# The opening of a graph-attention kernel: the first pair's terms by TensorE, the second quarter's values later

## The chip, the cores and the metric

The kernel runs on one core of a Trainium2 chip. The core has a matrix engine (TensorE, PE in the profile, with its weight loads as PEld), a vector engine (VectorE, DVE), an engine for copies and functions (ScalarE, ACT), a general engine (GpSimd, POOL) and a queue engine that issues transfers (SyncE, SP). Each works through its own queue in order and waits on semaphores for the others. The metric is the device time of one execution in microseconds (us).

## What is computed

Two graph-attention layers over 4096 nodes with 8 heads of 32 features, then one transformer layer over the same nodes, with the adjacency as the mask. The change touches only the start of the first graph-attention layer:

```python
def _gat_layer(x, adj_mat, W, a):
    O = W.shape[-1]
    Wh = jnp.einsum('nd,hdo->hno', x, W)
    src = jnp.einsum('hno,ho->hn', Wh, a[:, :O])
    dst = jnp.einsum('hno,ho->hn', Wh, a[:, O:])
    e = jax.nn.leaky_relu(src[:, :, None] + dst[:, None, :], 0.2)
    e = jnp.where(adj_mat[None, :, :] > 0, e, NEG_INF)
    alpha = jax.nn.softmax(e, axis=-1)
    out = jnp.einsum('hnm,hmo->hno', alpha, Wh)
    return jnp.transpose(out, (1, 0, 2)).reshape(N, -1)
h = jax.nn.elu(_gat_layer(x, adj_mat, W1, a1)) + x
out = jax.nn.elu(_gat_layer(h, adj_mat, W2, a2)) + h
```

Everything is float32; x is 4096 x 256 and adj 4096 x 4096 (int32).

## The kernel before

**How attention is computed.** The exponent of a leaky sum splits into two products, one for each sign of `src[n] + dst[m]`. So the kernel never makes the 4096 x 4096 scores. It compares `src` of a row n with `-dst` of a column m, gets a tile of signs in 8 bits, masks it with the adjacency, and multiplies the signs and the mask with scaled values of the columns on TensorE. The scaled values are `vst`, in two float16 halves that add up to the float32 number.

**Groups.** The work of a layer is cut into groups `(l, nb, p, g)`: layer, block of 1024 rows, pair of heads, and one eighth of the columns (four tiles of 128 nodes, 512 nodes). These eighths are numbered q in the preparation; the title of the change and this text call the first two quarter 0 and quarter 1. A group needs a tile `t8` of 128 x 2 x 4 x 1024 signs. `compare(i)` makes it for group i: for each of the four column tiles k and both heads j one comparison of 128 x 1024 numbers, on ScalarE (L1114) or on VectorE (L1116), and then one masking operation on VectorE (`mask`, L1129). One operand of a comparison is `s_b`, the row terms `src` of the block's 1024 nodes for the two heads, the same on all 128 partitions. The other is one number per partition, `-dst`, from `terms`. A group's matmuls are L1452; they add into six banks of the accumulator memory (bank0 to bank5) over the eight groups of a pair.

**Preparation of a quarter** (`preparation`, L980) makes the values of 512 nodes:

- features: four transposes of the rows of x for each half of the features (L991), and a copy by ScalarE (L1000, tile `g_ft`)
- values: for each of four tiles of 128 nodes two matmuls of 272 columns (`values_out`, L1005): 256 columns of values and 16 of terms. Then `values_in`: two exponentials, one more and a copy of the terms on ScalarE (L1018 to L1020); the largest value (L1023), the product (L1034) and 32 times the exponentials (L1040) on VectorE. For quarter 1 the product goes to `g_prod`, a pool of two buffers
- split: a cast to float16 (L1046, by ScalarE in the opening) and the rest by GpSimd (L1049). The GpSimd operation releases the `g_prod` buffer
- term rows: one transpose (L1054), a copy by ScalarE into `g_sr` (L1060), a pool with one buffer, and four DMAs to the DRAM tensor `s_d` (L1063).

**The mask's own path.** Adjacency units of 256 x 512 are loaded (`mask_load`, L858), clipped to 8 bits by VectorE (`mask_clip`, L867), transposed by TensorE (`turn_out`, L892, into one of two banks named turn), copied by ScalarE (`turn_in`, L898) and written to DRAM for later (L901). The three load buffers `g_adj` come free with the clips; each later clip issues one further load (`load_ahead`).

**The opening** (`begin`, L1280) sets by hand the order of PE, ACT, DVE and SP up to the first group. Before the change this order is: the loads; features of both quarters; the term weights; values of quarter 0 with clips between; quarter 0's term rows; values of quarter 1 with the splits of quarter 0; quarter 1's term rows; `s_fetch` (L1085), two DMAs that read `s_d` back from DRAM with each row repeated over 128 partitions; turns 0 to 3 with clips 4 to 7; `compare(0)`; turns 4 to 7 with the clips of the next column eighth; `compare(1)`. Then the groups follow. The first six groups each also prepare one further quarter: its features, values, term rows, turns and clips are laid between the group's matmuls by position (`side`), in an order that is the same for all engines, and `compare(i + 2)` runs there too.

Before `begin` two small tests run that use the turn banks: L833 and L834 on one, L840 to L846 on the other. They are outside the order written by hand.

Of the kernel before, what the change touches and what calls it, by code (L numbers as in the profile page):

```python
# [8 lines left out]
F32 = mybir.dt.float32  # L9
# [8 lines left out]
ALU = mybir.AluOpType  # L18
# [4 lines left out]
P = 128  # L23
# [661 lines left out]
UP = 32.0  # L685
# [66 lines left out]
def graph_attention(  # L752
# [62 lines left out]
    def turn_bank(shape, dtype):  # L815
        return ps.tile(shape, dtype, name="turn", tag="turn", bufs=2)

    spare = []

    def spare_bank():  # L820

        spare.append(0)
        return ps.tile([P, 512], F32, name=f"bank{(len(spare) - 1) % 6}")

# [153 lines left out]
    def preparation(l, q, bank, first=False):  # L980
# [32 lines left out]
        def values_in(t):  # L1013
            at = G * q + t
            pv = held.pop(("v", t))
            big = some.tile([P, 2, H], F32, name="g_big", bufs=4)
            for i, scale in enumerate((-1.0, -LRELU)):
                nc.scalar.activation(big[:, i, :], pv[:, D + H : D + 2 * H], AF.Exp, scale=scale)  # L1018
            nc.scalar.activation(L.r[:, at, :], pv[:, D : D + H], AF.Exp, scale=LRELU - 1.0)
            nc.scalar.copy(  # L1020
                L.terms[:, :, at, :], pv[:, D : D + 2 * H].rearrange("p (k h) -> p k h", k=2)
            )
            nc.vector.tensor_reduce(  # L1023
                L.tops[:, at : at + 1], pv[:, :D], AX.X, ALU.max, apply_absolute_value=True
            )

            if l == 0 and q != 1:
                if t == 0:
                    held["prods"] = ep.tile([P, G, H, 2, V1], F32, name="ev_broad")
                prod = held[t] = held["prods"][:, t]  # L1030
            else:
                prod = held[t] = some.tile([P, H, 2, V1], F32, name="g_prod")
            by_head = big.rearrange("p i h -> p h i").unsqueeze(3)
            nc.vector.tensor_tensor(  # L1034
                prod[:, :, :, :O],
                pv[:, :D].rearrange("p (h o) -> p h o", o=O).unsqueeze(2).to_broadcast([P, H, 2, O]),
                by_head.to_broadcast([P, H, 2, O]),
                op=ALU.mult,
            )
            nc.vector.tensor_scalar(prod[:, :, :, O:], by_head, UP, None, op0=ALU.mult)  # L1040

        def split(t):
            part = held.pop(t).rearrange("p h i v -> p h (i v)")
# [38 lines left out]
    def take(n):  # L1082
        return [step for _ in range(min(n, len(later))) for step in later.pop(0)]

    def s_fetch(l, nb, p):  # L1085
        s_b = s_p.tile([P, 2, W], F32, name="s_b")
        first, n = STARTS[l][nb] * P, TILES[l][nb] * P
        for j in range(2):
            row = s_d[l][2 * p + j : 2 * p + j + 1, first : first + n]
            nc.sync.dma_start(s_b[:, j, :n], spread(row, [[0, P], [1, n]]))  # L1090
        return s_b
# [5 lines left out]
    def compare(i):  # L1097

        l, nb, p, g = groups[i]
        L, s_b = layers[l], s_of[l, nb, p]  # L1100
        t8 = s8[i] = t_p.tile([P, 2, NW, G, HB], F8, name="t8")
        more = (7, 11, 15, 23, 27, 31) if l == 0 else (3, 7, 11, 15, 19, 23, 27)
        if apart(i):
            u8[i] = [rows_p.tile([P, NW, G, HB], F8, name="g_adj", bufs=3) for j in range(2)]

        def step(k):
            mt = g * G + k
            for j in range(2):
                to = t8[:, j, :, k, :]
                s = s_b[:, j, :].rearrange("p (w n) -> p w n", n=HB)  # L1110
                negd = L.negd[:, mt, 2 * p + j : 2 * p + j + 1]

                if (j == 1 or mt in more) and not (i == 0 and k == 0):
                    nc.scalar.activation(to.bitcast(I8), s, AF.Sign, bias=negd, scale=-1.0)  # L1114
                else:
                    nc.vector.tensor_scalar(  # L1116
                        to, s, negd, -1.0, op0=ALU.is_ge, op1=ALU.mult, saturate=False
                    )

        def mask():  # L1120
            both = t8.rearrange("p j w g n -> p j (w g n)").bitcast(I32)
            m32 = masks[l, nb][g].rearrange("p w g n -> p (w g n)").bitcast(I32)
            for j, u in enumerate(u8.get(i, ())):
                nc.vector.scalar_tensor_tensor(
                    u.rearrange("p w g n -> p (w g n)").bitcast(I32),
                    t8[:, j].rearrange("p w g n -> p (w g n)").bitcast(I32),
                    -1, m32, op0=ALU.bitwise_xor, op1=ALU.bitwise_and,
                )
            nc.vector.scalar_tensor_tensor(  # L1129
                both, m32.unsqueeze(1).to_broadcast(list(both.shape)), SIGNS, both,  # L1130
                op0=ALU.bitwise_or, op1=ALU.bitwise_and,
            )

        return [lambda k=k: step(k) for k in range(G)] + [mask]

    def pair_end(l, nb, p, ev):
# [143 lines left out]
    def begin():  # L1280

        weights_load(0)
        rows_ahead(0, 0)
        rows_ahead(0, 1)

        units = own[: 2 * 2 * NW]
        del coming[: len(units)]
        for k, u in enumerate(units):
            place = None
            if 3 <= k < 7:  # L1290
                place = mask_p.tile([P, 2, G * P], I32, name="mask")
            elif k == 7:
                place = t_p.tile([P, 2, G * P], I32, name="t8")
            mask_load(*u, place)

        def clip(k):
            mask_clip(*units[k], load=False)

        def turn(k):
            mask_turn(*units[k])  # L1300

        def both(use):
            use[0]()
            use[1]()

        (f_0, v_0, part_0, row_0), (f_1, v_1, part_1, row_1) = (
            preparation(0, q, spare_bank, True) for q in range(2)
        )
        for use in f_0 + f_1:
            both(use)  # L1310
        for step in weights_steps(0):
            step()
        for use in v_0[:2]:
            both(use)
        for k in range(2):
            clip(k)
            both(v_0[2 + k])
        both(row_0)
        for k in range(4):
            both(v_1[k])  # L1320
            part_0[k]()
            if k < 2:
                clip(2 + k)
            if k > 1:
                part_1[k - 2]()
        both(row_1)
        s_of[0, 0, 0] = s_fetch(0, 0, 0)
        rows_ahead(0, 2)
        for k in range(4):
            turn(k)  # L1330
            if k < 2:
                part_1[2 + k]()
            clip(4 + k)
        load_ahead(3)
        ahead = turns[0]
        for step in compare(0):
            step()
        for k in range(4, len(units)):
            turn(k)
            mask_clip(*ahead[k - 4])  # L1340
        for step in compare(1):
            step()
# [822 lines left out]
```

## Time and profile before

| | |
|---|---|
| time, median of 3 runs | 3174.34 us (3171.62 to 3174.59) |
| the profiled execution | 3169.78 us, span 3168.0 us |
| TensorE busy | 3073.6 us, 97% of the span |
| VectorE, ScalarE, GpSimd busy | 89%, 84%, 38% |
| granted TensorE clock, mean | 0.996 |
| first matmul of the first group | 40.33 us after the span's start |
| next group's first transposes | 59.94 us |

The page gives shares over the whole span; the opening is the first 1.3% of it. There the timeline is the view to use: one line for each run of like instructions on an engine, with its start, its length, the line of the program, what it writes and reads, how many, and in brackets how long the engine sat idle before it and what ended that. The view of stretches gives busy time by engine in a piece of the span, with the granted clock of TensorE. A float32 matmul stands in the trace as two records.

### The profile page before, as it was taken

How to read it: one execution, taken by the hardware profiler on the slowest of the kernel's cores; microseconds unless marked ns; L12 is line 12 of the kernel's file. 1: busy time of each engine (PE TensorE's matmuls, PEld its weight loads, DVE VectorE, ACT ScalarE, POOL GpSimd, SP SyncE). 2: the span in 40 equal slices, each digit the busy share in tenths (PEclk: the TensorE clock that was granted, in tenths of full speed). 3: DMA queues.
4: the chain of work that ended last, by engine and by line, in shares of the span. 5: the costliest groups of instructions: out<-in, count | busy, mean ns of one | idle time of the engine just before them, and what ended most of it. 6: DMA issues, size and time to landing. Idle time of an engine off the chain costs nothing. (4 is left out here: it accounts for less than half of the span.)

```text
span 3168.0 us, 139144 instructions
## 1 busy us (share of the span) xinstructions
PE 3073.6 (97%) x64076; PEld 2705.3 (85%) x64076; DVE 2809.0 (89%) x3201; ACT 2668.9 (84%) x3177; POOL 1197.6 (38%) x538
## 2 busy tenths in 40 slices
PE   6999999999989999999999999999999999999999
PEld 5899999999889999999985888888888888877766
DVE  7899999989899999999985999999999999998221
ACT  6899999999789999999965888888888888886332
POOL 3300000000330000000002998899988898997110
PEclk8999999999999999999999999999999999999999
DMA  8766555420310312121136010101011010111210
GB/s 256 214 198 206 165 188 152 150 87 22 102 53 23 96 56 86 32 68 56 46 111 173 14 41 18 37 21 34 28 27 33 22 50 8 47 60 56 69 35 22
DMA packets 212034, 250.35 MB, mean 79 GB/s; under 512 B 88240, under 2 KB 132784, under 8 KB 211440
## 3 DMA queue, kind: packets, MB, share of 16 engines
q1 hardware_dynamic: 211440, 241.36, 25.6%
q8 instruction: 503, 8.24, 1.1%
q14 instruction: 91, 0.75, 0.1%
HBM read 198.84 MB, written 42.47 MB: 76 GB/s over the span
## 5 line engine op out<-in xcount | busy, mean ns | idle before, releaser
L1452 PE MATMUL bank<-vst,t 128*128 128x132 f16 x16384 | 1450.7, 219 | 25.3 <-DVE t L1129 25.2
L1936 POOL TENSOR_TENSOR u_both<-u_e 128x1024 f32<-128x1024 f32 x448 | 1049.6, 2384 | 899.5 <-DMA u_k<-half_d 786.4
L1114 ACT ACTIVATE t<-s_b,g_terms 128x1024 int8<-128x1024 f32 x1231 | 1318.9, 1157 | 31.4 <-PE bank L1452 24.4
L1452 PE MATMUL bank<-vst,mask 128*128 128x66 f16 (+1 forms) x10296 | 1344.1, 206 | 0.0
L1452 PEld LDWEIGHTS <-t 128*128 128x128 fp8e4 x16384 | 1183.3, 96 | 39.7 <-DVE t L1129 29.6
L1818 DVE SCALAR_TENSOR_TENSOR u_e<-u_mask,u_ps 128x1024 f32<-128x1024 uint8 x1024 | 1166.1, 1215 | 15.1 <-ACT u_ps L1816 10.2
L1816 ACT ACTIVATE u_ps<-u_ps 128x1024 f32<-128x1024 f32 x1024 | 1030.2, 1009 | 139.7 <-PE u_ps L1809 44.6
L1452 PEld LDWEIGHTS <-mask 128*128 128x128 fp8e4 x10296 | 901.4, 98 | 0.0
L1129 DVE SCALAR_TENSOR_TENSOR t<-mask,t 128x2048 int32<-128x2048 int32 x256 | 589.0, 2301 | 61.3 <-ACT t L1114 51.4
L1809 PE MATMUL u_ps<-u_q,u_k 128*32 128x512 f16 x8192 | 637.4, 381 | 5.9 <-DVE u_e L1818 3.4
L1827 PE MATMUL u_av<-u_e,u_v 128*32 128x128 f32 x16384 | 603.1, 273 | 3.3 <-issue 3.3
L1827 PEld LDWEIGHTS u_av<-u_e,u_v 128*32 128x32 f32 x16384 | 489.4, 110 | 131.6 <-issue 4.8
L1116 DVE TENSOR_SCALAR t<-s_b,g_terms 128x1024 fp8e4<-128x1024 f32 x817 | 587.9, 752 | 2.6 <-DMA s_b<-s_d 2.6
L1049 POOL TENSOR_TENSOR vst<-g_prod,vst 128x528 f16<-128x528 f32 x36 | 59.5, 1669 | 748.2 <-DVE vst L1048 735.6
L1827 PE MATMUL u_dn<-u_both,u_ones 128*32 128x128 f32 x7168 | 282.4, 273 | 0.8 <-POOL u_both L1936 0.8
L1809 PEld LDWEIGHTS <-u_k 128*32 128x32 f16 x8192 | 230.1, 95 | 50.9 <-issue 9.9
L1827 PEld LDWEIGHTS u_dn<-u_both,u_ones 128*32 128x32 f32 x7168 | 214.1, 110 | 42.1 <-POOL u_both L1936 1.7
L2031 ACT ACTIVATE u_hid<-misc,n_b 128x512 f32<-128x512 f32 x64 | 43.9, 687 | 140.2 <-PE misc L2024 140.2
L2044 PE MATMUL misc<-u_k,u_hid 128*128 128x256 f32 x512 | 111.8, 379 | 0.0
L2024 PE MATMUL misc<-ln_cols,u_k 128*128 128x512 f32 x256 | 111.3, 593 | 0.5 <-ACT ln_cols L1548 0.5
L2044 PEld LDWEIGHTS misc<-u_k,u_hid 128*128 128x128 f32 x512 | 96.7, 190 | 13.3 <-issue 0.5
L2024 PEld LDWEIGHTS misc<-ln_cols,u_k 128*128 128x128 f32 x256 | 48.6, 190 | 58.5 <-issue 56.9
(167 smaller groups left out, 1825.0 us busy)
## 6 DMA issues: line engine op xcount, KB each, us to landing
g_adj<-in_adj_dram SPq DMA_DIRECT2D x123, 512.0 KB
s_b<-s_d SPq DMA_DIRECT2D x64, 512.0 KB
mask<-mask SPq DMA_DIRECT2D x128, 256.0 KB
u_mask<-mask SPq DMA_DIRECT2D x32, 512.0 KB
mask<-stage SPq DMA_DIRECT2D x48, 256.0 KB
half_d<-u_halves SPq DMA_DIRECT2D x32, 256.0 KB
u_q<-half_d SPq DMA_DIRECT2D x32, 256.0 KB
rows<-e_x SPq DMA_DIRECT2D x31, 256.0 KB
```

The source lines that it names most:

```text
L1049: nc.gpsimd.tensor_tensor(halves[:, :, 1, :], part, halves[:, :, 0, :], op=ALU.subtract)
L1114: nc.scalar.activation(to.bitcast(I8), s, AF.Sign, bias=negd, scale=-1.0)
L1116: nc.vector.tensor_scalar(to, s, negd, -1.0, op0=ALU.is_ge, op1=ALU.mult, saturate=False)
L1129: nc.vector.scalar_tensor_tensor(both, m32.unsqueeze(1).to_broadcast(list(both.shape)), SIGNS, both, op0=ALU.bitwise_or, op1=ALU.bitwise_and,)
L1452: nc.tensor.matmul(to, left, right, start=k not in opened, stop=last)
L1809: nc.tensor.matmul(ps[r * O : (r + 1) * O, j, :], k_st[c][:, 2 * u + j, at : at + O], q_st[:, h, :], start=True, stop=True,)
L1816: nc.scalar.activation(ps, ps, AF.Exp, scale=SCALE)
L1818: nc.vector.scalar_tensor_tensor(e, mask, 0.0, ps, op0=ALU.not_equal, op1=ALU.mult)
L1827: nc.tensor.matmul(to[j * O : (j + 1) * O, at], lefts[j], es[j // 2][:, j % 2, at], start=first and part == 0, stop=last and part == PARTS ...
L1936: nc.gpsimd.tensor_tensor(both, es_of[i - 1][u], es_of[i][u], op=ALU.add)
L2024: nc.tensor.matmul(ph, w1_sb[:, k, f * P : (f + 1) * P], hn[:, k, :], start=(k == 0), stop=(k == DC - 1),)
L2044: nc.tensor.matmul(po[:, :D], hid[:, f, at : at + P], w2_sb[:, f, :], start=(f == 0), stop=(f == FC - 1),)
```

## The change

- A new helper, `s_spread(q, j, bank)`, makes the row terms of 512 nodes for one head on all partitions: a matmul whose weights are one column of `w_ext` (the term weights of the head) repeated 128 times, with the features of the quarter as the moving operand. ScalarE copies the 128 x 512 result into `s_b`. Four of these replace the first `s_fetch`; the other pairs' terms still go through DRAM.
- Twelve float32 matmuls of the identity by itself (128 columns) into a turn bank stand at the head of TensorE's order. Nothing reads them.
- Quarter 0's values, splits and clips 0 to 3 are followed by turns 0 to 3, the four spreads, clips 4 to 7, three loads. Quarter 1's value matmuls stand behind the spreads on TensorE; their second halves (`values_in`), its splits and the term rows of both quarters stand behind `compare(0)` with its mask, ahead of turns 4 to 7 and `compare(1)`.
- `compare(0)` takes head 0's four tiles first, then head 1's; VectorE does the first two tiles of head 1 rather than one.
- In the opening L1040's multiply is done by ScalarE.
- Banks are given in a list written out, no longer in rotation; the load of quarter 2's rows is issued earlier.

```diff
+    def banks_of(order):
+        left = list(order)
+        def bank():
+            k = left.pop(0)
+            if k is None:
+                return turn_bank([P, 512], F32)
+            return ps.tile([P, 512], F32, name=f"bank{k}")
+        return bank
...
-            nc.vector.tensor_scalar(prod[:, :, :, O:], by_head, UP, None, op0=ALU.mult)
+            if first:
+                nc.scalar.mul(prod[:, :, :, O:], by_head, UP)
+            else:
+                nc.vector.tensor_scalar(prod[:, :, :, O:], by_head, UP, None, op0=ALU.mult)
...
+    def s_spread(q, j, bank):
+        L = layers[0]
+        pt = bank()
+        for c in range(DC):
+            nc.tensor.matmul(
+                pt,
+                L.w_ext[:, c, D + j : D + j + 1].to_broadcast([P, P]),
+                L.ft[q][:, c, :],
+                start=(c == 0),
+                stop=(c == DC - 1),
+            )
+        nc.scalar.copy(s_of[0, 0, 0][:, j, q * HB : (q + 1) * HB], pt)
...
-                if (j == 1 or mt in more) and not (i == 0 and k == 0):
+                if (j == 1 or mt in more) and not (i == 0 and k < 2):
...
+        if i == 0:
+            return [lambda k=k, j=j: step(k, (j,)) for j in range(2) for k in range(G)] + [mask]
...
-            preparation(0, q, spare_bank, True) for q in range(2)
+            preparation(0, q, banks_of(order), True)
+            for q, order in ((0, (0, 1, 4, 5, 0, 1, 2)), (1, (2, 3, None, None, 4, 5, 3)))
         )
+        pt = turn_bank([P, 512], F32)
+        for _ in range(12):
+            nc.tensor.matmul(pt[:, :P], ident_f, ident_f, start=True, stop=True)
         for use in f_0 + f_1:
             both(use)
         for step in weights_steps(0):
             step()
-        for use in v_0[:2]:
-            both(use)
-        for k in range(2):
-            clip(k)
-            both(v_0[2 + k])
-        both(row_0)
+        rows_ahead(0, 2)
+        clip(0)
         for k in range(4):
-            both(v_1[k])
-            part_0[k]()
-            if k < 2:
-                clip(2 + k)
-            if k > 1:
-                part_1[k - 2]()
-        both(row_1)
-        s_of[0, 0, 0] = s_fetch(0, 0, 0)
-        rows_ahead(0, 2)
+            both(v_0[k])
+            if k > 0:
+                part_0[k - 1]()
+            if k in (1, 2):
+                clip(k)
+        clip(3)
+        part_0[3]()
         for k in range(4):
             turn(k)
-            if k < 2:
-                part_1[2 + k]()
-            clip(4 + k)
+        s_of[0, 0, 0] = s_p.tile([P, 2, W], F32, name="s_b")
+        s_bank = banks_of((2, 3, 0, 1))
+        for j in range(2):
+            for q in range(2):
+                s_spread(q, j, s_bank)
+        for k in range(4, len(units)):
+            clip(k)
         load_ahead(3)
         ahead = turns[0]
-        for step in compare(0):
+        comparing = compare(0)
+        for use in v_1:
+            use[0]()
+        for step in comparing[:G]:
+            step()
+        for step in comparing[G:]:
             step()
+        for k in range(4):
+            v_1[k][1]()
+            if k > 0:
+                part_1[k - 1]()
+        both(row_0)
+        both(row_1)
+        part_1[3]()
         for k in range(4, len(units)):
             turn(k)
             mask_clip(*ahead[k - 4])
```

## The prediction

> **What bounds the kernel now.** I read the page first, then the stretches, then ScalarE's, SyncE's and TensorE's timelines of the first 62 us, where the change lies.
>
> From the page, TensorE's share of the chain that ended last, and two of the costliest groups:
>
> ```profile
> PE 45%; POOL 0%; DVE 0%; issue 0%; ACT 0%; ACTq 0%; DVEq 0%
> ...
> L2024 PE MATMUL misc<-ln_cols,u_k 128*128 128x512 f32 x256 | 111.3, 593 | 0.5 <-ACT ln_cols L1548 0.5
> ```
>
> No engine but TensorE has a share that shows, and its page row has it busy for 97% of the span. Nothing behind the opening waits for a clock time: a group starts when the one before it is done. So a microsecond won or lost before the first group should stand at the end, and 6.3 us (0.2% of 3174) is about what this measurement can tell from no change.
>
> Stretches (length, then busy PE, PEld, DVE, ACT, POOL, granted clock, DMA share, GB/s):
>
> ```profile
> 20.80:23.80 3.00, 0.77 (x10) 0.61 (x10) 3.00 (x8) 2.23 (x9) 3.00 (x3) 0.99 0.70 135
> 23.80:40.30 16.50, 3.31 (x24) 2.42 (x23) 11.92 (x17) 8.74 (x15) 5.66 (x5) 0.50 0.75 219
> 40.30:44.20 3.90, 3.87 (x30) 3.75 (x31) 1.89 (x3) 3.90 (x4) 0.00 (x0) 0.50 0.54 169
> 60.00:74.30 14.30, 12.34 (x152) 10.62 (x151) 12.74 (x23) 11.36 (x31) 6.42 (x4) 1.00 0.87 268
> ```
>
> Until 40.3 TensorE is nearly idle. Its clock halves 3.0 us after the last value matmul (20.8) and is back only after 3.9 us of unbroken work. A later group of the opening takes 14.3 us with no engine full: three queues hand work on in a fixed order.
>
> ScalarE's timeline (start, length, line, what, count, idle before):
>
> ```profile
> 23.67 0.25 ACT L1060 COPY g_sr<-bank 32x128 f32<-32x128 f32 x1
> ...
> 34.73 3.23 ACT L1114 ACTIVATE t<-s_b,g_terms 128x1024 int8<-128x1024 f32 x3 [5.04 <-DMA s_b<-s_d]
> ...
> 40.09 5.29 ACT L1114 ACTIVATE t<-s_b,g_terms 128x1024 int8<-128x1024 f32 x5
> 45.28 1.05 ACT L1000 COPY g_ft<-turn 128x512 f32<-128x512 f32 x2
> ```
>
> This is the queue to watch. The terms' row leaves at 23.67, returns over DRAM, and both heads are on the partitions at 34.73. The second comparison starts at 40.09, and behind it waits the copy (45.28) that group 0's features need. I take that 40.09 as the mark.
>
> SyncE and TensorE:
>
> ```profile
> 23.95 1.58 SPq L1063 DMA_DIRECT2D s_d<-g_sr  x4
> ...
> 27.04 0.47 SPq L1496 DMA_DIRECT2D n_be<-in_L_gnn_be_dram  x1
> 27.68 0.82 SPq L1090 DMA_DIRECT2D s_b<-s_d  x2
> ```
>
> ```profile
> 8.09 1.94 PE L991 MATMUL bank<-ident,g_rows 128*128 128x128 f32 x8 [8.09 <-DMA g_rows<-in_x_dram]
> ...
> 59.94 0.60 PE L991 MATMUL turn<-ident,g_rows 128*128 128x128 f32 x4
> ```
>
> Four row DMAs land by 27.68, 2.15 us after the last was issued (25.53). A transpose takes about 0.22 us at 8.09 and 0.11 at 59.94: at 8 us the array ran at half speed, whatever the clock column says for that early time. Value tiles (L1005) go from 1.8 us to 0.91 each at 13.45.
>
> **The change, part by part**, as shifts of the 40.09 mark.
>
> *1. Up to the spread.* Twelve f32 matmuls of 128 columns, two records each, at 0.21 at half speed: 5.1 us from 1.45 (the identity) to 6.6, under the wait for rows that ends at 8.09. They cost nothing; without that cover, 5.1. They may raise the clock: it rose at 13.45, 5.4 us after work began, so 5.1 us may or may not do. If it does, transposes and first values win 2.2 us; bounds 0 and 2.2, I take half. Then VectorE needs, per value tile, 0.34 + 0.60 = 0.94 us (L1023, L1034; L1040 has left it) four times, and two clips of 0.60 between: from 14.11 to 19.1. ScalarE casts (0.54) and copies turns 0 and 1 (0.53 each), which free the two banks for turns 2 and 3 (0.45): the spread, queued behind turn 3, starts at 21.2, less 1.1: 20.1.
>
> *2. The spread.* Head by quarter: four results of two f32 matmuls, two records each, 512 columns: 16 x 0.435 us (111.3/256 above) = 6.96 at full speed; up to 9.5 if a broadcast column keeps records from overlapping (16 x 0.593), which I don't take as 0.435 is what a row of such matmuls showed. From the last value (about 15.3) to 20.1 TensorE has only 16 short transposes, longer than the 3.0 us after which the clock fell: so half speed at first, for the 3.9 us of the row, loss 1.95 (bounds 0, and 2.7 for 5.4 us). The two s_b loads (1 MB) that fall away free nothing that waits: the quarter's own adjacency tiles had landed by 30.7, when their last clip ran without a wait. The copy adds 0.69. Head 1 is there at 20.1 + 6.96 + 1.95 + 0.69 = 29.7, against 34.73: 5.0 won.
>
> *3. First comparisons.* ScalarE has two rather than three: 1.05 + 1.14, then the mask (L1129) 2.29 and hand-overs 0.07: masked at 34.25, against 40.27. 6.0 won; VectorE's six comparisons (0.66) hide, four of them under head 1's spread.
>
> *4. What now stands behind the mask.* In the old order quarter 1's values lay under the DRAM trip. Now ScalarE must do them before turn 4's copy, and every step waits for another engine. From the mask's end: VectorE's tile 0, 0.94; cast 0.54 (at 1.53); GpSimd's subtraction 1.35 (opening's mean for g_prod): 2.9. Only then is one of the two g_prod buffers free, and ScalarE itself waits there, as L1040's multiply now sits in its queue (0.1). Cast 1 (3.55), GpSimd (4.9), multiply, cast 2 (5.55). Row 0's copy 0.16 (finished at 5.8), four issues on SyncE 1.37, landing 2.15: 9.3. Row 1's copy writes the same single g_sr buffer, so it waits for that landing; then 0.16, cast 3 0.54: 10.05. Turns 4 to 7: 2.2 with one wait for TensorE. Second comparison at 34.25 + 12.3 = 46.55. Before, it started 0.18 ahead of the mask's end. So the shift is 46.55 - 40.09 = +6.5. The landing is bounded by 0 and 2.15; SyncE stood still for 0.17 us just before the s_b issue, so I take 2.15. GpSimd's rows span 1.14 to 1.67: -0.4 to +0.6. The eight moved multiplies took VectorE 3.1 us (L1040, 0.17 to 1.08 each); small operations of that size follow each other on ScalarE at 0.06 to 0.1, so beyond the two waits they cost under 0.5, which I leave out.
>
> *5. Queues moved past.* Rows for quarter 2 and the three loads go out earlier, the eight row DMAs later: group 1's last adjacency load, behind them, is issued at about 45.3 and not 41. In the old run its lateness held VectorE 3.19 us. Now VectorE's three comparisons (2.0) end before ScalarE's five (5.3), and the mask comes about 2.9 us earlier after the mark. TensorE then waits no longer for VectorE's product in group 0 (a 0.66 us wait); ScalarE's 1.69 us wait for it may go too. Gain 0 to 2.35; I take TensorE's own, 0.7.
>
> **Sum:** +6.5 - 0.7 = +5.8 us. On the profiled execution (3169.78 run, 3168.0 span) that is 3175.6; the median shown is 4.6 above it: **3180.1**. Bounds: low 5.8 - 1.1 - 1.95 - 2.15 - 0.4 - 1.65 = -1.5; high 5.8 + 1.1 + 0.75 + 2.5 + 0.6 + 0.7 = +11.5. Its own range: 3172.8 to 3185.8.
>
> [...]
>
> **Rivals.**
>
> *Warm-up in the way (slower).* The 12 matmuls need one of two turn banks, and the two start-up tests in the code ahead use the same two. If the bank is theirs until VectorE reads it after the weights (9.0), the matmuls run from 9.1 to 14.2 and features start 6.1 late, at full speed (2.6 won): 3.5 instead of -1.1, so +10.4: 3184.7. For it: L834 ran at 10.10. Against it: the old trace put the tests behind eight transposes, though first in the code, so code order doesn't bind.
>
> *Short tail (faster).* One mechanism: ScalarE's tail behind the mask costs only its work, as buffers free themselves in time. Its own busy time there is about 4 x 0.54 + 2 x 0.3 + 0.3 for quarter 1 and 2.2 for turns: 5.3, and with tile 0's 0.94 it is 6.2 instead of 12.3: +6.5 - 6.1 = +0.4. Group 0, which took 19.6 us (40.33 to 59.94) against 14.3, then starts with its masks early and a fast clock; if it too takes 14.3, -5.3, and with part 1's other half -1.1: -6.0; with the spread at full speed too, -8. I put it at 3167. For it: group 0's excess is in the trace. Against it: the g_prod wait showed even before (0.7 and 0.78 us on VectorE). It decides below a tail of about 7 us.
>
> *It cancels.* The trip saved and the tail pay each other exactly (tail of 6.5): 3174.3.
>
> **Chances and range.** Forecast 60%, of which half beyond 6.3 us, as the sum is near it and the open terms reach further up; warm-up in the way 20%, all slower; short tail 14%, faster; cancels 6%. So slower 0.50, within 0.2% 0.36, faster 0.14. Range 3169 to 3187: it reaches past the slow rival and half-way to the short tail.
>
> **What would show it.** Right: ScalarE idle behind the first mask, waiting for GpSimd, then 3 us before the second g_sr copy; its second comparison near 46.5; s on the partitions near 30; clock 0.5 at the spread's start. Part 1 is wrong if transposes at 8.1 don't take 0.11 or 0.22, or come after 14. The prediction falls if the mark comes before 40, or if the group that starts near 60 has kept nothing of the shift.

## The result, and the profile after

| | before | changed |
|---|---|---|
| time, median of 6 runs each, side by side | 3172.93 us (3169.19 to 3174.59) | 3190.82 us (3189.45 to 3194.68) |
| ratio, with its 95% interval | 1 | 1.0062 [1.0051, 1.0072] |
| profiled execution, span | 3169.78 us, 3168.0 us | 3192.24 us, 3189.4 us |

The change costs 17.9 us. The forecast was 5.8 us, with a range that ended 12.7 us above the median it started from. The direction was right, the size was not.

The same points of the opening in both traces, with the forecast between them (us after the span's start):

| | before | forecast | changed |
|---|---|---|---|
| first transposes of the features (TensorE) | 8.09 | 8.09 | 17.26 |
| spread starts | - | 20.1 | 28.62 |
| head 1's terms on all partitions | 34.73 | 29.7 | 37.4 |
| first mask done | 40.27 | 34.25 | 41.92 |
| second comparison starts on ScalarE (the mark) | 40.09 | 46.55 | 53.01 |
| next group's transposes | 59.94 | +5.8 | 72.88 |

From the page of the changed kernel: busy time by engine, the instruction queue (packets, MB, share), and the shares of the chain that ended last.

```profile
PE 3090.6 (97%) x64116; PEld 2716.9 (85%) x64116; DVE 2809.5 (88%) x3194; ACT 2670.7 (84%) x3188; POOL 1197.4 (38%) x538
...
q8 instruction: 503, 8.24, 1.1%
...
PE 48%; DVE 3%; ACT 2%; issue 1%; DMA 0%; SPq 0%; DVEq 0%; ACTq 0%
```

VectorE and ScalarE now have shares of the chain, 3% and 2%; before, none but TensorE had one that shows. And "issue", time in which an engine waited for nothing that the profile shows, has come up to 1%. These shares don't tell a slower kernel from a faster one: experiment 9, below, the fastest kernel measured here, has PE 47%, DVE 3%, ACT 2% and issue 1%.

The stretches of the changed kernel (same columns as before):

```profile
12.10:17.40 5.30, 5.23 (x26) 5.26 (x27) 0.28 (x3) 0.00 (x0) 0.00 (x0) 1.00 1.05 388
...
28.60:36.80 8.20, 8.20 (x20) 3.80 (x18) 4.88 (x7) 2.63 (x6) 0.38 (x1) 0.87 0.73 225
41.90:52.30 10.40, 2.13 (x18) 1.86 (x19) 6.88 (x12) 4.82 (x19) 4.92 (x4) 0.62 0.02 4
...
73.00:87.30 14.30, 12.35 (x152) 10.63 (x151) 12.73 (x23) 11.36 (x31) 6.42 (x4) 1.00 0.70 234
```

In the first row TensorE is busy for the whole stretch while VectorE, ScalarE and GpSimd do next to nothing: those are the twelve identity matmuls, and everybody waits for them. (24 records in 5.25 us are 0.22 us each; the 16 of the transposes right behind them, in 1.91 us, are 0.12 each. So the matmuls ran at about half speed, though the clock column has 1.00 there.) The third is the tail behind the first mask: 10.4 us in which no engine is full. The last is a later group, the same as before within 0.01 us of TensorE's time.

TensorE's and VectorE's timelines of the changed kernel, around the late start:

```profile
9.20 0.27 PE L845 MATMUL turn<-g_ident_h,g_bits 128*128 128x128 f16 x1 [6.62 <-DVE g_ident_h L811]
12.17 5.25 PE L1336 MATMUL turn<-ident 128*128 128x128 f32 x24 [2.71 <-DVE checks L839]
17.26 1.91 PE L996 MATMUL bank<-ident,g_rows 128*128 128x128 f32 x16
```

```profile
11.27 0.70 DVE L872 TENSOR_SCALAR adj<-g_adj 128x1024 fp8e4<-128x1024 int32 x1 [2.12 <-DMA g_adj<-in_adj_dram]
11.88 0.15 DVE L839 TENSOR_SCALAR checks<-turn 128x1 f32<-128x1 f32 x1
```

The brackets tell the story. The matmuls (L1336) write a turn bank. The start-up check on VectorE (L839) still had to read that bank, and in VectorE's queue it stood behind clip 0 (L872), which waited for its adjacency until 11.27. So 24 records that were to run from 1.45 began at 12.17, and the features began behind them at 17.26 and not at 8.09.

ScalarE's timeline of the changed kernel, behind the mask, and SyncE's:

```profile
42.89 0.63 ACT L1054 CAST vst<-g_prod 128x528 f16<-128x528 f32 x1 [2.52 <-DVE g_prod L1039]
...
44.78 0.23 ACT L1046 ACTIVATE g_prod<-g_big 128x16 f32<-128x16 f32 x1 [0.99 <-POOL vst L1057]
...
47.42 0.25 ACT L1068 COPY g_sr<-bank 32x128 f32<-32x128 f32 x1
50.09 0.25 ACT L1068 COPY g_sr<-bank 32x128 f32<-32x128 f32 x1 [2.42 <-DMA s_d<-g_sr]
...
53.01 5.29 ACT L1136 ACTIVATE t<-s_b,g_terms 128x1024 int8<-128x1024 f32 x5
```

```profile
47.70 3.95 SPq L1071 DMA_DIRECT2D s_d<-g_sr  x8
51.75 0.55 SPq L863 DMA_DIRECT2D g_adj<-in_adj_dram  x1
```

Each wait in a bracket is one that the forecast's step 4 named: the product, GpSimd holding a buffer, the single term-row buffer until its DMAs have landed. Behind the eight row DMAs the late adjacency load goes out at 51.75.

The opening thus accounts for 12.9 us (72.88 - 59.94 = 12.94). That shift stands through both graph layers, 12.65 in the middle (the 129th masking operation, 889.83 against 877.18) and 13.44 at the last (1628.00 against 1614.56). The rest appears where nothing was changed, in the transformer's attention stage. From the first to the last of its sixteen copies into u_den, 1101.69 us before (1801.80 to 2903.49) have become 1108.98 (1815.88 to 2924.86). TensorE's timeline there, the changed kernel and then the one before:

```profile
1887.17 0.52 PE L1865 MATMUL u_dn<-u_both,u_ones 128*32 128x128 f32 x9 [0.86 <-issue]
...
2034.85 0.52 PE L1865 MATMUL u_dn<-u_both,u_ones 128*32 128x128 f32 x10 [0.59 <-issue]
...
2182.90 0.53 PE L1865 MATMUL u_dn<-u_both,u_ones 128*32 128x128 f32 x11 [0.96 <-issue]
...
2852.28 1.04 PE L1847 MATMUL u_ps<-u_q,u_k 128*32 128x512 f16 x7 [4.83 <-issue]
```

```profile
2608.26 0.75 PE L1827 MATMUL u_dn<-u_e,u_ones 128*32 128x128 f32 x19 [0.24 <-issue]
...
2755.51 0.86 PE L1827 MATMUL u_dn<-u_e,u_ones 128*32 128x128 f32 x24 [0.36 <-issue]
...
2832.56 0.86 PE L1827 MATMUL u_av<-u_e,u_v 128*32 128x128 f32 x24 [1.32 <-issue]
```

Once in about 147 us, a block of that stage, TensorE stops for half a microsecond to one, and no other engine is named. Before, these stops were at most 0.36 us and in front of other work. Near the stage's end comes a longer one, 4.83 us against 1.32. All stops over 0.15 us add up to 7.9 us in the changed kernel and 2.2 before, 5.7 of the stage's 7.3 us. Behind the longest one the clock was at half speed for 6.8 us, where the kernel before has no drop at all:

```profile
2850.20:2856.90 6.70, 4.62 (x68) 3.81 (x71) 1.59 (x2) 2.52 (x3) 6.70 (x4) 0.50 0.58 198
```

That is room enough for the other 1.6 us, though no run separates them.

### The profile page after: what moved, and what is told of

It is laid out like the page before. It is cut to its first block, busy times and chain, and to the rows that moved or that the text cites. A ratio compares the mean times of both kernels' runs of the same rounds, so it can differ in the third digit from the quotient of the medians.

```text
span 3189.4 us, 139221 instructions
## 1 busy us (share of the span) xinstructions
PE 3090.6 (97%) x64116; PEld 2716.9 (85%) x64116; DVE 2809.5 (88%) x3194; ACT 2670.7 (84%) x3188; POOL 1197.4 (38%) x538
## 3 DMA queue, kind: packets, MB, share of 16 engines
q8 instruction: 503, 8.24, 1.1%
## 4 chain that ended last, share of the span: by engine, by line
PE 48%; DVE 3%; ACT 2%; issue 1%; DMA 0%; SPq 0%; DVEq 0%; ACTq 0%
PE u_ps L1847 15%; PE u_av L1865 14%; PE u_dn L1865 8%; PE misc L2082 3%; PE misc L2062 3%; PE misc L1785 2%; ACT t L1136 1%; DVE t L1151 1%; DVE t L1138 1%; PE misc L2023 1%; PE misc L1804 1%; PE misc L1583 0%; DVE g_adj L1146 0%; ACT ev_broad L1500 0%; DVE u_e L1856 0%
## 5 line engine op out<-in xcount | busy, mean ns | idle before, releaser
L1847 PE MATMUL u_ps<-u_q,u_k 128*32 128x512 f16 x8192 | 642.2, 382 | 11.6 <-issue 7.3
```

What stands on the lines that cost most here:

```text
L1847: nc.tensor.matmul(ps[r * O : (r + 1) * O, j, :], k_st[c][:, 2 * u + j, at : at + O], q_st[:, h, :], start=True, stop=True,)
```

## The experiments

Theory A: the opening lost its time to the identity matmuls and to the tail. For the attention stage two answers were set against each other: the stops come with a late opening or are chance (rivals D and G), or they belong to TensorE's instruction stream (theory F). All medians stand beside runs of the kernel before on the same chip.

**1. The changed kernel without the identity matmuls.**

```diff
-        pt = turn_bank([P, 512], F32)
-        for _ in range(12):
-            nc.tensor.matmul(pt[:, :P], ident_f, ident_f, start=True, stop=True)
```

> The changed kernel without its twelve identity matmuls; everything else of the change stays. Theory A (the identity matmuls stood in the way of the features, and the tail behind the first mask costs about 11 us as traced): features at 8.1 us at half speed, spread from about 21, second comparison on ScalarE at about 46.5 against 40.09 in the kernel before and 53.01 with the matmuls, so the opening keeps +6.5 us. If what the changed kernel loses later, in the attention stage (some 5 us of its median), comes with the late opening and not with the rest of the change, the median is 3179 to 3181; if it belongs to the rest of the change, 3184 to 3186. Rival B (the features were late for another reason, rows or clips ahead of them): features stay after 15 us and the median stays near 3190.

Measured: 3178.87 us beside 3171.64, ratio 1.0023 [1.0013, 1.0034]. TensorE's and ScalarE's timelines of this kernel:

```profile
7.71 1.94 PE L996 MATMUL bank<-ident,g_rows 128*128 128x128 f32 x8 [7.71 <-DMA g_rows<-in_x_dram]
...
20.51 8.88 PE L1098 MATMUL bank<-g_ft,g_w_ext 128*128 128x512 f32 x16
```

```profile
45.63 5.29 ACT L1136 ACTIVATE t<-s_b,g_terms 128x1024 int8<-128x1024 f32 x5
```

Features at 7.71, spread at 20.51, the mark at 45.63 (+5.5). Theory A holds, B falls: by these two profiles 7.4 us of the mark are the matmuls' (53.01 - 45.63). And the median fell by more, by 10.7 us in its distance to before (17.9 - 7.2).

**2. The matmuls in a bank that nobody waits for, ahead of the tests.**

```diff
+    pt = ps.tile([P, 512], F32, name="bank5")
+    for _ in range(12):
+        nc.tensor.matmul(pt[:, :P], ident_f, ident_f, start=True, stop=True)
     tiny = keep.tile([P, 2], F16, name="g_tiny")
```

> The changed kernel with the twelve identity matmuls in a bank of the values instead of a turn bank, and in the code ahead of the two start-up tests, so that they wait for the identity alone. Theory A: they run from about 1.5 to 6.7 us, the features follow the second test at about 9.5 us at full speed (the clock has not yet fallen after 2.6 us without work), values from about 11.5; second comparison at 45 to 46, so +5 to +6 in the opening, and a median of 3178 to 3180, about 1 below the kernel without the matmuls. Rival C (the matmuls don't hold the clock over the gap): features from 9.5 at half speed, 1.4 later than without them, and a median 1 to 2 above that kernel's.

Measured: 3183.87 us, ratio 1.0043 [1.0029, 1.0057]. TensorE's timeline, its opening and then two places in the attention stage:

```profile
1.47 5.49 PE L834 MATMUL bank<-ident 128*128 128x128 f32 x24 [1.47 <-POOL ident masks.py:199]
...
8.91 0.22 PE L848 MATMUL turn<-g_ident_h,g_bits 128*128 128x128 f16 x1 [1.95 <-DVE g_ident_h L811]
8.96 1.92 PE L999 MATMUL bank<-ident,g_rows 128*128 128x128 f32 x16
...
1881.61 0.49 PE L1865 MATMUL u_dn<-u_both,u_ones 128*32 128x128 f32 x9 [1.07 <-issue]
...
2029.88 0.52 PE L1865 MATMUL u_dn<-u_both,u_ones 128*32 128x128 f32 x10 [1.21 <-issue]
```

The opening went as theory A said: matmuls from 1.47, features at full speed (16 records in 1.92 us) over a gap of 2 us, mark at 45.47. That is 0.16 us ahead of experiment 1, where the granted clock rose early, 2.75 us after the first transpose. In experiment 7, whose opening is experiment 1's up to that point, it rose 4.6 us after it, and the first comparison on ScalarE began at 31.38, against 30.04 in experiment 1 and 29.88 here. So by these profiles the warm-up is worth 0.2 to 1.5 us, depending on when the clock would have risen without it. Rival C falls. Yet the median is 5 us *above* experiment 1. Both kernels keep step up to the end of the layers (last masking operation at 1621.40 and 1621.44). They part by 2.0 us before the first copy into u_den and by 6.5 in the attention stage, 1110.91 us here and 1104.38 in experiment 1. The stops stand where the changed kernel has them, in front of the same work with the same count (x9, x10). The two have the same number of TensorE records, experiment 1 has 24 fewer. From here on the stream was the suspect.

**3. The kernel before with the twelve matmuls alone.** They stand in a turn bank at the head of TensorE's order, as in the change.

> The kernel before with the twelve identity matmuls of the change in a turn bank and nothing else of it. Theory A: the matmuls wait for VectorE's start-up check (10.1 us), run from about 10.3 to 15.6, features at 15.6 at full speed, first values on VectorE at 19 instead of 14.11; second comparison at 45 instead of 40.09, so +5 us and a median of 3177 to 3179. In the changed kernel they cost more (9 us at the features) since there the check stood on VectorE behind a clip that waited for its adjacency until 11.27. Rival D (the attention stage loses 5 us more whenever the opening ends late): 3182 to 3184.

Measured: 3182.16 us, ratio 1.0036 [1.0022, 1.0050]. TensorE and ScalarE:

```profile
9.47 5.00 PE L1311 MATMUL turn<-ident 128*128 128x128 f32 x24
...
14.31 1.91 PE L991 MATMUL bank<-ident,g_rows 128*128 128x128 f32 x16
```

```profile
42.84 5.30 ACT L1114 ACTIVATE t<-s_b,g_terms 128x1024 int8<-128x1024 f32 x5
```

Without a clip ahead of the check the matmuls start at 9.47 and not at 12.17: 2.7 us of the changed kernel's delay are the clip's. The mark is 2.75 us late, not 5. The median is 10.5 us above, as rival D said, but the profiled execution (3176.86) was the lowest of its five, so it shows only part of that: the attention stage took 1105.62.

**4. The spread alone, in the old order.**

```diff
-        s_of[0, 0, 0] = s_fetch(0, 0, 0)
+        s_of[0, 0, 0] = s_p.tile([P, 2, W], F32, name="s_b")
+        for j in range(2):
+            for q in range(2):
+                s_spread(q, j, spare_bank)
```

These lines stand ahead of quarter 1's term row.

> The kernel before with the trip over DRAM replaced by the four spreads, in the old order: quarter 1's values and splits stay ahead of the first comparisons, the spreads follow quarter 1's values on TensorE, their copies stand on ScalarE ahead of quarter 1's term row. No identity matmuls, no change to the comparisons. Theory A (what the change lost is the identity matmuls and the tail, not the spread): the spread runs from about 21 to 28, ScalarE's four copies (0.55 each) end at about 32 where the DRAM trip ended at 34.7, second comparison at 37 to 38.5, so -2 to -3 us and a median of 3169 to 3171. Rival E (the spread itself costs as much as the trip, as its copies stand in ScalarE's queue): second comparison at 40 or later, median 3172 to 3176.

Measured: 3173.29 us, ratio 1.0005 [0.9996, 1.0014]. ScalarE:

```profile
35.48 5.29 ACT L1128 ACTIVATE t<-s_b,g_terms 128x1024 int8<-128x1024 f32 x5
```

The mark is 4.6 us early, better than expected, and rival E falls. But the median did not move. In the trace the last masking operation of the layers is still 2.7 us early (1611.89 against 1614.56). The first copy into u_den is 0.9 late: in between TensorE waited 3.70 us for u_e, where the kernel before waited 2.30, and stopped 2.98 us on "issue", before 1.67. The attention stage behind it takes 1104.55, 2.9 us more. So the gain went in three places: 1.9 us in the layers, 3.5 ahead of the stage, 2.9 in it. Rival D falls too, since here the opening was early and the loss came all the same.

**5. The kernel before with 20 identity matmuls (40 records) in TensorE's idle time.**

```diff
+        def pads(n):
+            pt = ps.tile([P, 512], F32, name="bank5")
+            for _ in range(n):
+                nc.tensor.matmul(pt[:, :32], ident_f, ident_f[:, :32], start=True, stop=True)
...
         load_ahead(3)
+        pads(10)
...
             mask_clip(*ahead[k - 4])
+            if k == 5:
+                pads(10)
```

> The kernel before with 20 identity matmuls (40 records) of 32 columns, read by nobody, put where TensorE stands idle: ten behind turn 3, ten behind turn 5. So TensorE's instruction stream is as much longer ahead of the attention stage as in the changed kernel, and the opening is not held up. Theory F (the 4 to 7 us that the changed kernel, the one with the matmuls in a bank of their own and the kernel before with the matmuls lose behind the opening are stalls of TensorE's instruction stream at fixed places in the stream, near matmul records 33583 + 4222 k; more instructions ahead put other work on these places): second comparison at 40.1 as before, stalls of about 1 us in each block of the attention stage, median 3176 to 3178 beside 3171.6. Rival G (chance of the executions, or a late opening): median within 1.5 us of before.

Measured: 3177.75 us beside 3170.74, ratio 1.0019 [1.0010, 1.0028]. TensorE in the attention stage:

```profile
1871.72 0.52 PE L1835 MATMUL u_dn<-u_both,u_ones 128*32 128x128 f32 x10 [0.68 <-issue]
...
2019.91 0.53 PE L1835 MATMUL u_dn<-u_both,u_ones 128*32 128x128 f32 x11 [1.10 <-issue]
```

The opening was not held up (first mask at 37.52, before 37.98; last masking operation at 1613.81, before 1614.56), and still 7 us are lost. The stops are within two records of where the changed kernel has them. Rival G falls.

**6. The spread with 112 short matmuls, 128 records more than before in all.** 40 were put ahead of the start-up tests, 56 behind turns 1 to 3, 16 behind turn 5, each with two columns.

> The kernel with the spread in the old order, with 112 short matmuls (112 records, 2 columns) in TensorE's idle time: 40 at the start, 56 behind turns 1 to 3, 16 behind turn 5. With the spread's 16 records that makes 128 records, that is 256 instructions of 64 bytes, as many as one 16 KB packet of the instruction queue holds. Theory F: the attention stage's work stands against the packets as it does in the kernel before, its stalls go back to the size there (0.1 to 0.6 us a block), and the opening keeps its gain: second comparison at 35 to 37, median 3167 to 3170, below both kernels. Rival G: 3173 as without the short matmuls, or above it.

The packet there is an estimate, and goes back to the page of the kernel before: 503 packets and 8.24 MB on the instruction queue are 16.4 KB a packet, and shared among TensorE's 128,152 instructions (64,076 matmul records and as many weight loads) 64.3 bytes each.

Measured: 3170.33 us, ratio 0.9996 [0.9987, 1.0005], at the edge of what was expected. The attention stage is back at 1101.37. But the 40 at the start came behind the first transposes (8.05 us) and held up the features, and the mark came at 37.41, 1.9 later than in experiment 4.

**7 and 8. The tail.** Both leave the identity matmuls out. Experiment 7 gives g_sr two buffers; experiment 8, besides, puts quarter 1's products into the pool of four.

```diff
-            sr = some.tile([G * H, P], F32, name="g_sr", bufs=1)
+            sr = some.tile([G * H, P], F32, name="g_sr", bufs=2)
...
-            if l == 0 and q != 1:
+            if l == 0:
```

> The changed kernel without its identity matmuls, and with two buffers for g_sr instead of one, so that the copy of the second term row doesn't wait for the first row's DMAs to land. Theory A (the tail behind the first mask is made of the waits that the profile names): the wait of 2.4 us before the second g_sr copy goes, second comparison at 43.2 instead of 45.63, median 2 to 3 below the kernel with one buffer (3178.9): 3176 to 3177, TensorE's stream being the same. Rival H (the wait is covered by the turns, which need TensorE anyway): nothing gained.

> As the last kernel, and quarter 1's products go to the pool of four tiles that quarter 0 uses (ev_broad) instead of the pool of two, so that GpSimd's subtraction no longer holds up ScalarE's multiply and VectorE's product. Theory A: the two waits of 0.99 us on ScalarE go too, second comparison at 41 to 41.5, median 3174 to 3175. Rival I (GpSimd, at 1.3 to 1.7 us a tile, sets the tail with any number of buffers): second comparison stays at 43.

Measured: 3179.29 us, ratio 1.0023 [1.0014, 1.0032], and 3174.62 us, ratio 1.0009 [1.0000, 1.0018]. The clock rose later in the profiles of these two than in experiment 1 (the second half of the feature transposes took 1.91 us and not 1.48, and the spread began at 21.4 and 21.6 instead of 20.5), so the tail is counted from the first comparison on ScalarE to the second: 15.59 us in experiment 1, 13.08 in 7, 11.23 in 8. The 2.5 and 1.9 us that the waits had been given are there, and H and I fall for the mark. In the median experiment 7 shows nothing of it. One part of the reason is on SyncE, experiment 7:

```profile
41.66 2.73 SPq L1071 DMA_DIRECT2D s_d<-g_sr  x8
44.49 0.55 SPq L863 DMA_DIRECT2D g_adj<-in_adj_dram  x1
```

Counted like the tail, the late adjacency load goes out 13.11 us after the first comparison and in experiment 1 14.32 after it (44.36 - 30.04): 1.2 us earlier, where the mark is 2.5. It still stands behind all eight row DMAs, and group 1's mask, which needs it, comes only 1.3 us earlier by the same count. The later clock took the rest in the profile (51.84 against 51.75 on the span's own count). Experiment 8 keeps more of its gain: the mask at 50.03.

**9. Experiment 6 without the fault: 8, 8 and 96 short matmuls behind turns 1, 2 and 3.**

> The spread in the old order again, with the 112 short matmuls all in TensorE's idle time behind turns 1 to 3 (8, 8 and 96), none at the start, where 40 of them had come behind the first transposes and held the features up by some 2 us. At 0.028 us each 96 take 2.7 us of the 3.2 in which TensorE waited there. Theory F: second comparison at 35.5 to 36 as without them, attention stage as in the kernel before (1101 to 1102 us from the first to the last of its sixteen divisor copies, 1104.6 without the short matmuls), median 3166 to 3168, below both kernels. Rival G: 3170 to 3173.

Measured: 3168.33 us beside 3172.17, ratio 0.9990 [0.9981, 0.9999]. TensorE:

```profile
29.32 2.54 PE L1323 MATMUL bank<-g_ident_h 128*128 128x2 f16 x96
34.18 1.06 PE L892 MATMUL turn<-g_ident_h,adj 128*128 128x128 f16 x8 [1.60 <-ACT mask L898]
```

They fit into the idle time (1.60 us of it are left), the mark is at 35.77, the attention stage takes 1101.57. This is faster than both kernels, though the gain is small and its interval ends just below 1.

**10. The whole changed kernel with 88 short matmuls between the two term rows**, which makes its 40 records 128.

```diff
         both(row_0)
+        pads(88)
         both(row_1)
```

> The changed kernel, whole, with 88 short matmuls between the two term rows, where TensorE waits 5.3 us: its 40 records more than the kernel before become 128, one packet of the instruction queue. Theory F: the opening keeps its +12.9 us (second comparison at 53), the attention stage comes down from 1109 to 1101 to 1103 us, median 4 to 6 below the changed kernel's: 3184 to 3187. Rival G: 3190.

Measured: 3183.73 us, ratio 1.0038 [1.0025, 1.0052]. ScalarE:

```profile
53.52 5.29 ACT L1136 ACTIVATE t<-s_b,g_terms 128x1024 int8<-128x1024 f32 x5
```

The opening is as late as ever (+13.4 at the mark), the attention stage takes 1102.38, and 11.6 us are left of 17.9. So by these medians 6.3 us of what the change cost came from the length of its TensorE code and from nothing it does. Kernels from two rounds of runs are compared here, and their intervals just touch, so the size is rough.

**11. Half a packet: the spread with 48 short matmuls behind turn 3.**

> The spread in the old order with 48 short matmuls behind turn 3: 64 records more than the kernel before, half a packet. Theory F says only that the stalls keep their places in the stream and meet other work, so that the attention stage may take anything from 1101 to 1111 us; if its size runs on evenly from 16 records (1104.6) over 24 (1105.6) to 40 (1106.6 to 1111), it is over 1106 here and the median 3174 to 3178. If it is 1101 to 1103, the loss belongs to a narrow stretch of shifts, and the median is 3167 to 3169.

Measured: 3176.16 us, ratio 1.0017 [1.0008, 1.0026], attention stage 1110.77. The loss runs on over the half packet; it isn't a narrow stretch.

All eleven kernels, the one before and the changed one, by the records that TensorE has more than the kernel before ahead of the attention stage:

| records more | attention stage, us |
|---|---|
| 0 (before) | 1101.7 |
| 16 (experiments 1, 4, 7, 8) | 1104.4, 1104.6, 1102.8, 1102.5 |
| 24 (3) | 1105.6 |
| 40 (5, changed, 2) | 1106.6, 1109.0, 1110.9 |
| 64 (11) | 1110.8 |
| 128 (6, 9, 10) | 1101.4, 1101.6, 1102.4 |

Each of these times is from one execution, up to 5.3 us from its kernel's median, so neighbours can't be ranked by them. Two other counts give the same order. The stops over 0.15 us add up to 2.2 us with no record more, 3.5 to 4.9 with 16, 6.2 with 24, 7.4 to 10.3 with 40, 10.7 with 64 and 2.3 to 2.7 with 128. And what a median is above the kernel before, less the shift of the mark, is 1.2 to 6.3 us with 16 records, 5.0 to 7.8 with 24 to 64, and -1.9 to 2.3 with 128.

## Why the prediction was wrong, step by step

**Step 1 failed.** It said of the twelve matmuls, from 1.45 to 6.6 "under the wait for rows": "They cost nothing; without that cover, 5.1." The cover was never there. The spread began 8.5 us later than forecast (28.62, not 20.1). The rival "Warm-up in the way" had the mechanism and a price of 6.1 us at the features. It was talked down with "code order doesn't bind", and order was beside the point: the matmuls waited for a *bank*, and got it only when its reader had run (L839, 11.88 to 12.03; the matmuls from 12.17). It was also priced too low, because the reader's own queue was not looked at: the change puts clip 0 ahead of that check, 2.7 us by experiment 3. The gain that step 1 gave the warm-up (1.1 us, half of 2.2) is 0.2 to 1.5 in experiment 2, and the features there could not start before the second start-up test (8.96 instead of 7.71).

**The clock of step 1.** The rows gave the warm-up an even chance, since the clock had risen after 5.4 us. The changed kernel and experiment 2 show transposes at full speed (0.12 us a record) right behind 5.25 us of matmuls and 2 us after 5.49 us of them, so it worked there. In the four kernels with the twelve matmuls (the changed one, experiments 2, 3 and 10) the granted clock rose 3.9 to 5.4 us after they began. But in the kernels without them the rise came 2.7 to 6.2 us after the first transpose (experiments 4 and 6), so that it must work isn't shown.

**Step 2 was right.** Results 2 to 4 came 1.72 us apart, four records at 0.43; the first took 3.0, with the granted clock at 0.50 up to 30.72, so the slow clock cost 1.3 us rather than 1.95. The broadcast column cost nothing more: the forecast's row had 0.435. **Step 3 was right:** 4.5 us from the last copy to the masked tile, as forecast. **Step 4 was right in each wait** and 1.2 us too long (11.1 against 12.3): the second term-row copy came 8.2 us behind the mask and not 9.3. **Step 5** gave 0.7 us back; nothing came. The load went out at 51.75, 1.3 us ahead of the mark, where 45.3 had been forecast against 46.55, just as near to it. But VectorE then waited 5.80 us for it and not 3.19, and the shift at the next group's transposes is 12.94, the mark's own 12.92.

The mark by these terms: 8.52 (step 1) - 0.84 (step 2 with its copy) - 0.01 (step 3) - 1.21 (step 4) = 6.46, which is 53.01 - 46.55. With step 5's 0.7 the opening is 7.1 us worse than the sum.

**The premise under the sum failed too**: "a microsecond won or lost before the first group should stand at the end". It stood through both layers. Then the attention stage added 7.3 us in the profiled execution and some 5 to 6 in the medians (17.9 - 12.9; 6.3 by experiment 10), and neither forecast nor rivals had a term for it. In experiment 4 the same took 2.9 us of what the spread had gained, and 3.5 more were lost just ahead of that stage.

## What to carry to other kernels

Work that is meant to fill an idle stretch must find its output buffer free (here the matmuls began at 12.17 and not at 1.45): ask who reads that buffer last, and what stands ahead of the reader in its queue. When a microsecond won early doesn't arrive at the end, or one is lost where nothing was changed, look for "issue" stops on the bound engine, and try the same kernel with its instruction stream made longer by a whole packet (here 128 matmul records), in idle time; that tells the edit's own effect from that of its length. The spread itself was a good change for the opening, 4.6 us at the mark: it only had to keep quarter 1's values where they were hidden. At the end of the kernel its gain showed with the padding alone (experiment 9), and small.

## What the runs showed of the hardware that was not expected

**This kernel's instruction stream has places where TensorE stops, and they stay put while the work moves.** The kernel before has 128,152 TensorE instructions and 503 packets on the instruction queue, 254.8 to a packet. By this estimate, which takes the queue to carry TensorE's stream and little else, a packet is some 127 matmul records with their weight loads. The pages bear it out: with 16 to 64 records more (the changed kernel, experiments 1 to 5 and 11) there are still 503 packets and 8.24 MB, with 128 more (experiments 6, 9 and 10) 504 and 8.26 MB. 128 records, 256 instructions, are counted as a packet below. Counted in the trace, the stops of the attention stage come before matmul records 33,584, 37,806 and 42,028 in the changed kernel and in experiment 2, 33,582, 37,804 and 42,026 in experiments 3 and 5, 33,581, 37,803 and 42,025 in experiments 4 and 11. That is within three records of each other, though up to 64 were added ahead, and 4,222 apart: 8,444 instructions, close to 33 such packets (8,448). With 128 records more the stops that show are those of the kernel before, one packet on (50,597 and 54,819 in experiment 6, where before has 50,470 and 54,692). So by these counts the places go by packets. Counted within its packet, and allowing for the 2 records by which 4,222 falls short of 33 packets, the place is the same in all thirteen traces: of the stage's 79 waits of TensorE over 0.15 us, 74 lie within five records of each other, and the other five wait for GpSimd. With the work that falls on such a place the size of the stop changes, from nothing that shows to 1.8 us in the blocks, and to 4.8 once at the stage's end (changed kernel, at 2852). Why mostly one place in 33 packets shows was not tried.

**Here a wait of 2 us was followed by 3.4 us at half speed or by none, by where it fell.** Between the 129th and the 145th masking operation, around the change of layers, the kernels took 115.7, 116.9 or 118.3 us, with no, one or two drops of the clock. Stretches of the kernel before, and of experiment 1:

```profile
905.00:912.00 7.00, 6.94 (x113) 6.67 (x111) 6.68 (x8) 7.00 (x9) 0.00 (x0) 1.00 0.36 77
949.00:955.00 6.00, 6.00 (x119) 6.00 (x117) 5.86 (x7) 6.00 (x10) 0.00 (x0) 1.00 0.01 3
```

```profile
908.00:912.00 4.00, 4.00 (x50) 4.00 (x48) 3.96 (x7) 4.00 (x5) 0.00 (x0) 0.57 0.14 30
952.00:956.00 4.00, 4.00 (x48) 4.00 (x47) 3.90 (x4) 1.93 (x4) 0.00 (x0) 0.57 0.46 151
```

A mean of 0.57 over 4 us is 3.4 us at half speed (the granted clock of the changed kernel is 0.50 from 959.15 to 962.56). The changed kernel had one such drop and experiment 10, with nearly the same times, none; experiment 9 had two, 2.5 us of the 4.2 by which it was ahead at the 129th operation. Just ahead of the two first rows TensorE waits for a mask, equally long in both kernels (experiment 1, then before):

```profile
907.15 0.29 PE L1487 MATMUL bank<-vst,t 128*128 128x132 f16 x2 [2.03 <-DVE t L1151]
```

```profile
902.44 0.29 PE L1452 MATMUL bank<-vst,t 128*128 128x132 f16 x2 [2.03 <-DVE t L1129]
```

Within each trace the changes of the granted clock lie whole multiples of 3.413 us apart (in the changed kernel at 17.07, 27.31, 30.72 and so on to 959.15, 962.56, 1737.39, 1740.80; in experiment 1 at 10.46, 17.29, 24.11 and so on to 908.17, 911.58, 952.54, 955.95). So each trace can be cut, from its changes, into stretches of 3.413 us, and how a wait falls on these goes with which kernel is hit. Between the two operations every trace has three waits of TensorE of 1.8 to 2.1 us, 39 in all. The 14 that had 1.94 us or more inside one stretch were followed by a drop at that stretch's end; the 25 that had at most 1.85 in one were not. (Elsewhere in the changed kernel 1.97 us in a stretch left the clock up, so the border isn't exact.) In the two lines above, experiment 1's wait lies in one stretch whole, and of the wait in the kernel before 0.56 us fall in one and 1.47 in the next.

Open: at the start of the attention stage TensorE's first wait for u_e took 1.0 to 2.4 us in ten profiles and 3.5 to 3.8 in three (changed kernel, experiments 2 and 4), and this does not follow the number of records.
